# Row LSTM after a group norm: the second row of both halves issued in the steady order instead of in sequences of its own

## The chip, the core and the metric

The kernel runs on one core of one Trainium2 chip. A time is the device time of one execution in microseconds (us). Before the change the median of three runs is 2032.22 us (2031.02 to 2032.76). One more execution was taken with the hardware profiler; it took 2030.92 us, and its trace spans 2029.1 us.

## What is computed

The input x has 8 images of 96 channels, 128 rows and 128 columns, all in 32-bit floats. It is group-normalised; a masked convolution along the row gives four gate inputs for each pixel; then an LSTM walks down the rows, and its hidden state h is convolved along the row with three taps. The result is added to x. Cut to what matters:

```python
its = conv(groupnorm(x), W_is * mask) + b_is          # 96 -> 384 channels, 1x3, along the row
def step(carry, row_in):
    h, c = carry
    gates = conv(h, W_ss) + b_ss + row_in             # 96 -> 384 channels, 3 taps, along the row
    f, i, o = sigmoid(...), sigmoid(...), sigmoid(...)
    g = tanh(...)
    c_new = f * c + i * g
    h_new = o * tanh(c_new)
    return (h_new, c_new), h_new
x = x + scan(step, rows of its)
```

Rows depend on each other through h and c. The images don't.

## The kernel before

**Halves and steps.** The eight images are two halves of four. A *half step* n is one row of one half: n = 2 x row + half, so steps 0 and 1 are the first row of both halves, steps 2 and 3 the second row, and the last step is 255. Step n needs h of step n-2. While one half's gates are computed, TensorE works on the other half. "h(n)", "vf(n)" and so on below are what belongs to step n.

**What a step consists of.** The 384 gate channels are three banks of PSUM, A, B and C, of 128 channels. Even and odd pixels of a row are kept apart, and each bank has two halves of 256 columns for them. The operands of a step are made from h of the row above: `F` (`difference`, tile vf, on VectorE, L585), `S` (`total`, tile vs, VectorE, L573) and `D` (`shifted`, tile vd, GpSimd, L589). TensorE then writes, for each bank, the products of x (`P`, `Q`, weights wx; `E`, weights wt) and of h (`1` from vs, `2` from vf, `0` and `3` from vd); all are line L442. In between, ScalarE copies half a bank out with the bias (`cp`, L508) and VectorE adds and subtracts it back (`lo` L512, `hi` L516), so that even and odd pixels come out of fewer products; only then do `0`, `3` and `E` go into the bank. The gates follow: `ta` (tanh, ScalarE, L520), `si` (sigmoid, ScalarE, L527), `fg` (f times c, VectorE, L532), `gt` (i times g, L537), `ce` (L547), `th` (tanh of c, ScalarE, L552) and `ou` (h, VectorE, L560). `re` (L607, GpSimd) adds h to x for the output.

**The order is written out by hand.** Each engine executes its instructions in the order in which the code lists them. `do(n, names)` lists parts of step n. In a name, `'` means step n-1, `+` step n+1 and `*` step n+2; `F`, `S` and `D` always mean the operands of two steps later. A part that is already listed is skipped. From step 4 on, every step is listed by one string, `PERIOD`:

```python
    PERIOD = (
        "2A hiC' siA' D'' 1B 1A taA' 2B fg' 3C' 1A 0C' re'' taB' 2A 2B EC' 1B cpA 0C' 2C W loA cpB "
        "3C' 1C siB' loB PB+ QA+ hiA taCb' 2C hiB taCa' 0A gtb' 1C siC' gta' EA 0B ceb' cpC 3A PA+ "
        "cea' thb' PC+ 3B loC tha' QC+ oub' EB oua' QB+ 3A F' 3B 0A S' 0B"
    )
```

It mixes products of step n with the gates of step n-1 and with the x products of step n+1. `W` lists GpSimd's preparation of later rows of x (`prepare(n-1)`: normalising images into the tiles xs and hx, L297, L315, L316). Gates with a trailing a or b are done for the even or the odd pixels alone.

**Row groups.** With `by_lanes=True` products are listed in *pieces* of 64 of the 128 contraction rows: a product of h is two pieces and is named twice in `PERIOD`; a product of x has its operand twice in the tile, and one piece is enough. The two 64-row groups of the array work side by side. `Lanes.take` chooses a group so that both get as many pieces; where a bank was last written from the other group, `lanes.wait` has TensorE wait for that product. Without `by_lanes`, a product of h is one matmul over 128 rows (`whole`), and one of x goes to a group fixed by its bank (`own`).

**Around the change.** The statistics of x take the first 134 us or so. Steps 0 and 1 and the products of step 2 are listed by hand in the lines above L936 and are not touched. Then come L936 to L945, which list steps 2 and 3; the two `PERIOD` calls in them add what was still missing (GpSimd's `prepare`, residuals, and the products P and Q of step 4). At L946 the loop over steps 4 to 255 begins.

Of the kernel before, what the change touches and what calls it, by code (L numbers as in the profile page):

```python
# [21 lines left out]
def kernel(  # L22
# [335 lines left out]
    last = NT * NH - 1  # L358
# [299 lines left out]
    def prepare(n):  # L658
        if n not in worked:
            worked.add(n)  # L660
            for part, *args in work(n):
                part(*args)

    def finish(n):
        prepare(n)
        row, s = divmod(n, NH)
        k, r = divmod(row, R)
        if r == R - 1:
            store(s, k, R - 1 if k + 1 == NB else 0, R)
            if k + 2 < NB:  # L670
                load(s, k + 2)
        elif r == R - 2 and k + 1 == NB:
            store(s, k, 0, R - 1)
# [4 lines left out]
# [5 lines that stand above are left out]
# [10 lines left out]
    def half_step(n):  # L693
        if n not in steps:
            steps[n] = HalfStep(n)
        return steps[n]

    def do(n, names, by_lanes=False):

        for name in names.split():  # L700
            if name == "W":
                prepare(n - 1)
                continue
            at = n
            for mark, offset in (("'", -1), ("+", 1), ("*", 2)):
                at += offset * name.count(mark)
                name = name.replace(mark, "")
            pixels = PIXELS[name[-1]] if name[:-1] in SPLIT and name[-1] in PIXELS else ()
            whole_name = name[:-1] if pixels else name
            tile_ = whole_name[-1] if whole_name[-1] in order else ""  # L710
            part = whole_name[: len(whole_name) - len(tile_)]

            if part in ("S", "F", "D"):
                at += NH
            if not 0 <= at <= last:
                continue
            step = half_step(at)
            if name in step.done or whole_name in step.done:
                continue
            if by_lanes and (part in OWN or part in H_PRODUCTS) and (  # L720
                at < last or part in ("P", "Q") or (part, order[tile_]) in step.halves
            ):
                if step.piece(part, order[tile_]):
                    step.done.add(name)
                continue
            step.done.add(name)
            getattr(step, PARTS[part])(*([order[tile_]] if tile_ else []), *pixels)
            if by_lanes and part == "re":
                finish(at)
# [120 lines left out]
    n = m = 0  # L850
# [82 lines left out]
    finish(0)  # L933
    do(1, "gt th 0+A 3+A 0+B 3+B 0+C 3+C ou F S D re")
    finish(1)
    do(2, "taA siA taB fg siB taC")  # L936
    do(3, "2A 1A 2B 1B PC QC 2C 1C cpA cpB loA loB hiA hiB")
    do(2, "gt ce siC th")
    do(3, "cpC")
    do(2, "ou")  # L940
    do(3, "loC hiC EA EB EC 0A 3A 0B 3B 0C 3C")
    do(2, "F S D")
    do(2, PERIOD, by_lanes=True)
    do(3, PERIOD, by_lanes=True)
    do(3, "taA siA taB fg siB taC gt ce siC th ou F S D")  # L945
    for n in range(4, last + 1):  # L946
        do(n, PERIOD, by_lanes=True)
    do(last, "cpA cpB cpC loA hiA loB hiB loC hiC 0A 3A EA 3B 0B EB", by_lanes=True)
    do(last, "taA siA 0C 3C EC siB taB fg taC siC gt oua' oub' re'", by_lanes=True)
# [63 lines left out]
```

## Time and profile before

| | before |
|---|---|
| median of three runs | 2032.22 us |
| the runs | 2031.02 to 2032.76 us |
| profiled execution | 2030.92 us |
| its span | 2029.1 us |
| busy: TensorE, VectorE, ScalarE, GpSimd | 95%, 75%, 74%, 72% of the span |
| TensorE, instructions in the trace | 16912 matmuls |
| mean granted TensorE clock | 0.997 of full speed |

The profile comes from one execution. PE is TensorE's matmuls, PEld its weight loads, DVE VectorE, ACT ScalarE, POOL GpSimd, SPq the queue that issues DMAs. One product of the code shows as two matmul records. A line of the timeline has the start in us from the span's start, the time until the last of the merged instructions ends, the engine, the line, the operation, the tile written and the tiles read, partitions x elements, and how many records are merged; a bracket names the idle time before it and what ended it. `64*128` is a matmul over 64 contraction rows, `128*128` over all 128.

### The profile page before, as it was taken

The page shows a single profiled execution, that of the slowest core. Times are in us where ns is not written, and L with a number is a line of the kernel's source. Part 1 is how long each engine was busy: PE and PEld are TensorE (multiplying, and loading weights), DVE is VectorE, ACT ScalarE, POOL GpSimd, SP SyncE. Part 2 cuts the span into 40 slices and gives each one's busy share as a digit, 9 for nine tenths or more (in the row PEclk, how much of TensorE's full clock was granted, in tenths as well). Part 3 has the DMA queues.
Part 4 walks back from the last instruction along what each step waited for, and adds up shares of the span by engine and source line. Part 5 has one row for each costly group of instructions (what it writes and reads, how often), then busy time and mean ns, then how long its engine had stood idle before and what let it go on. Part 6 is the DMA issues. An engine that isn't in the chain of part 4 may idle for free.

```text
span 2029.1 us, 44784 instructions
## 1 busy us (share of the span) xinstructions
PE 1925.3 (95%) x16912; PEld 1830.0 (90%) x16912; DVE 1526.6 (75%) x3990; ACT 1493.7 (74%) x3157; POOL 1469.6 (72%) x1712
## 2 busy tenths in 40 slices
PE   0289999999999999999999999999999999999998
PEld 0267999999999999999999999999999999999997
DVE  5776777777777777777777777777777777777776
ACT  4775777777777777777777777777777777777776
POOL 3347777777777777777777777777777777777752
PEclk9999999999999999999999999999999999999999
DMA  9993433443343344333433443343344334434411
GB/s 378 424 314 79 108 95 95 115 115 94 79 100 98 92 114 115 100 84 89 113 91 100 116 115 85 82 106 95 95 115 115 95 79 99 105 91 109 115 32 32
DMA packets 103382, 237.11 MB, mean 117 GB/s; under 512 B 5952, under 2 KB 8896, under 8 KB 97280
## 3 DMA queue, kind: packets, MB, share of 16 engines
q1 hardware_dynamic: 103168, 234.25, 42.5%
q8 instruction: 135, 2.21, 0.5%
q14 instruction: 79, 0.65, 0.1%
HBM read 183.90 MB, written 50.33 MB: 115 GB/s over the span
## 4 chain that ended last, share of the span: by engine, by line
PE 92%; DMA 4%; ACT 2%; DVE 1%; issue 0%; SPq 0%; POOL 0%; DVEq 0%; POOLq 0%
PE ps L442 92%; DMA piece<-in_x_dram 3%; DMA xs<-in_x_dram 1%; ACT piece L216 1%; PE ps L174 0%; ACT piece L217 0%; DVE bst L876 0%; ACT g L520 0%; ACT hx L295 0%; ACT piece L295 0%; DVE hx L560 0%; DVE ps L516 0%; ACT ps L527 0%; ACT xs L216 0%; ACT xs L217 0%
## 5 line engine op out<-in xcount | busy, mean ns | idle before, releaser
L442 PE MATMUL ps<-vd,wl 64*128 64x256 f32 (+1 forms) x6084 | 1390.3, 380 | 0.3
L442 PEld LDWEIGHTS ps<-vd,wl 64*128 64x128 f32 (+1 forms) x6084 | 1028.3, 187 | 46.4 <-issue 2.1
L442 PE MATMUL ps<-vs,wm 64*128 64x256 f32 (+1 forms) x3046 | 773.8, 380 | 5.0 <-POOL vs L573 4.2
L442 PE MATMUL ps<-vf,wm 64*128 64x256 f32 (+1 forms) x3046 | 765.5, 377 | 1.1 <-DVE vf L585 1.1
L527 ACT ACTIVATE ps<-ps 96x512 f32<-96x512 f32 x766 | 441.7, 577 | 356.3 <-PE ps L442 348.0
L442 PE MATMUL ps<-xs,wx 64*128 64x256 f32 x3080 | 637.2, 378 | 11.2 <-POOL xs L315 11.1
L589 POOL TENSOR_TENSOR vd<-hx 128x512 f32<-128x512 f32 x257 | 266.2, 1036 | 398.4 <-PE ps L442 391.5
L442 PEld LDWEIGHTS ps<-xs,wx 64*128 64x128 f32 x3080 | 493.3, 188 | 15.1 <-POOL xs L315 11.5
L520 ACT ACTIVATE g<-ps 32x512 f32<-32x512 f32 x1019 | 468.0, 482 | 30.7 <-PE ps L442 10.4
L442 PEld LDWEIGHTS ps<-vf,wm 64*128 64x128 f32 (+1 forms) x3046 | 475.4, 187 | 13.1 <-DVE vf L585 1.5
L442 PEld LDWEIGHTS ps<-vs,wm 64*128 64x128 f32 (+1 forms) x3046 | 460.6, 186 | 21.6 <-POOL vs L573 5.3
L512 DVE TENSOR_TENSOR ps<-m,ps 128x256 f32<-128x256 f32 x768 | 325.7, 425 | 192.2 <-ACT m L508 181.9
L442 PE MATMUL ps<-xs,wt 64*128 64x256 f32 x1530 | 453.1, 377 | 2.5 <-DVE ps L516 2.4
L508 ACT ACTIVATE m<-ps,wl 128x256 f32<-128x256 f32 x766 | 360.9, 473 | 92.1 <-PE ps L442 85.6
L532 DVE TENSOR_TENSOR ps<-ps,c 96x512 f32<-96x512 f32 x254 | 176.7, 696 | 238.9 <-PE ps L442 231.0
L607 POOL TENSOR_TENSOR x<-x,hx 96x512 f32<-96x512 f32 x255 | 330.0, 1294 | 6.8 <-DVE hx L560 6.7
L516 DVE TENSOR_TENSOR ps<-m,ps 128x256 f32<-128x256 f32 x768 | 300.8, 422 | 1.3 <-PE ps L442 1.2
L442 PEld LDWEIGHTS ps<-xs,wt 64*128 64x128 f32 x1530 | 279.7, 186 | 15.5 <-DVE ps L516 3.2
L316 POOL TENSOR_TENSOR xs<-xw 128x512 f32<-128x512 f32 (+1 forms) x254 | 270.0, 1063 | 0.0
L297 POOL TENSOR_SCALAR hx<-x,rstd,nmr 32x384 f32<-32x384 f32 (+2 forms) x312 | 224.6, 720 | 32.9 <-DMA x<-in_x_dram 0.8
L297 POOL TENSOR_SCALAR xw<-xr,rstd,nmr 128x512 f32<-128x512 f32 x252 | 205.0, 814 | 7.2 <-DVE nmr L289 6.7
L537 DVE TENSOR_TENSOR g<-ps,g 96x256 f32<-96x256 f32 (+1 forms) x505 | 188.7, 413 | 5.4 <-ACT g L520 5.4
(91 smaller groups left out, 1218.2 us busy)
## 6 DMA issues: line engine op xcount, KB each, us to landing
xr<-in_x_dram SPq DMA_DIRECT2D x124, 512.0 KB, 6.6
x<-in_x_dram SPq DMA_DIRECT2D x63, 768.0 KB, 6.0
out_dram<-x SPq DMA_DIRECT2D x62, 768.0 KB, 4.6
xs<-in_x_dram SPq DMA_DIRECT2D x30, 1024.0 KB, 12.5
piece<-in_x_dram SPq DMA_DIRECT2D x16, 1024.0 KB, 12.3
x<-in_x_dram SPq DMA_DIRECT2D x62, 256.0 KB, 3.2
xs<-in_x_dram SPq DMA_DIRECT2D x4, 512.0 KB, 8.2
out_dram<-x SPq DMA_DIRECT2D x2, 576.0 KB, 3.7
```

The costliest lines, as they stand in the source:

```text
L297: return engine.tensor_scalar(dst, src, scale, shift, ALU.mult, ALU.add)
L316: nc.gpsimd.tensor_sub(differences, strided(xw[:, 0, :], 0, [(W + 1, n), (J, 2), (1, J)]), strided(xw[:, 0, :], J + 1, [(W + 1, n), (0, 2) ...
L442: made = nc.tensor.matmul(self.ps[a][:, bass.ts(half, HB)][:, cols], weights[rows, bass.ts(a, P)], rhs[rows, cols], start=new, stop=False, ...
L508: nc.scalar.activation(self.m1[a], m1, AF.Identity, bias=column)
L512: nc.vector.tensor_add(self.ps[a][:, 0:HB], self.m1[a], self.ps[a][:, HB:])
L516: nc.vector.tensor_sub(hi, self.m1[a], hi)
L520: nc.scalar.activation(self.part(g, lo, hi, t), self.part(ps, lo, hi, t), AF.Tanh)
L527: nc.scalar.activation(gate, gate, AF.Sigmoid)
L532: nc.vector.tensor_mul(f, f, self.c)
L537: nc.vector.tensor_mul(to, i, g)
L589: diff = nc.gpsimd.tensor_sub(self.operand("vd", 2)[:, :, lo:hi], strided(h, 1, [(BH * JP - 1, 2), (JP, hi - lo), (1, J)]), strided(h, 0, ...
L607: (nc.gpsimd if 2 * row + s < last else nc.vector).tensor_add(xo, xo, self.h)
```

## The change

The hand-written sequences of steps 2 and 3 (L936 to L945) go, and the loop over `PERIOD` starts at step 2:

```diff
     finish(0)
     do(1, "gt th 0+A 3+A 0+B 3+B 0+C 3+C ou F S D re")
     finish(1)
-    do(2, "taA siA taB fg siB taC")
-    do(3, "2A 1A 2B 1B PC QC 2C 1C cpA cpB loA loB hiA hiB")
-    do(2, "gt ce siC th")
-    do(3, "cpC")
-    do(2, "ou")
-    do(3, "loC hiC EA EB EC 0A 3A 0B 3B 0C 3C")
-    do(2, "F S D")
-    do(2, PERIOD, by_lanes=True)
-    do(3, PERIOD, by_lanes=True)
-    do(3, "taA siA taB fg siB taC gt ce siC th ou F S D")
-    for n in range(4, last + 1):
+    for n in range(2, last + 1):
         do(n, PERIOD, by_lanes=True)
```

What stays to be listed at n = 2 is little, since the products of step 2 are already listed above: `W` and the products `PC+` and `QC+` of step 3. At n = 3 the products of step 3 are listed in 64-row pieces, mixed with the gates of step 2 and with P and Q of step 4. The last products of step 3's bank C (`3C'`, `0C'`, `EC'`), its `hiC'` and its gates come at n = 4, mixed with the products of step 4. The end of the kernel (L948 on) has the same text. The number of arithmetic operations is the same except that twelve 128-row products become twenty-four 64-row pieces, and that the gates taC, gt, ce, th and ou of steps 2 and 3 are split into even and odd pixels.

## Prediction

> A *cycle* n runs here from TensorE's first product of vf(n) to its first of vf(n+1): one half step in the loop.
>
> **What bounds the kernel now.** First the page: what carries the chain that ended last.
>
> ```profile
> PE 92%; DMA 4%; ACT 2%; DVE 1%; issue 0%; SPq 0%; POOL 0%; DVEq 0%; POOLq 0%
> ```
>
> TensorE carries it nearly throughout. The chain in order of time shows where it doesn't, after the statistics:
>
> ```profile
> 157.85 0.44 DVE ps L516
> 158.33 5.85 PE ps L442 x18
> ...
> 174.31 26.45 PE ps L442 x215
> ...
> 206.41 1807.24 PE ps L442 x16244
> ```
>
> The long stretch runs at 1807.24/16244 = 0.111 us a record; in the middle one it is 26.45/215 = 0.123. Just ahead of 158.33 TensorE waited for VectorE. The TensorE timeline of that place, with a first record of later cycles:
>
> ```profile
> 151.16 0.70 PE L442 MATMUL ps<-vf,wm 128*128 128x256 f32 x2 [1.06 <-DVE vf L585]
> ...
> 158.33 0.70 PE L442 MATMUL ps<-xs,wt 64*128 64x256 f32 x2 [2.43 <-DVE ps L516]
> 158.96 4.54 PE L442 MATMUL ps<-vd,wl 128*128 128x256 f32 x12
> 163.43 2.33 PE L442 MATMUL ps<-xs,wx 64*128 64x256 f32 x12
> 165.59 0.38 PE L442 MATMUL ps<-vf,wm 64*128 64x256 f32 x1
> ...
> 173.04 0.48 PE L442 MATMUL ps<-vf,wm 64*128 64x256 f32 x1
> ...
> 182.29 0.48 PE L442 MATMUL ps<-vf,wm 64*128 64x256 f32 x1
> ...
> 190.54 0.38 PE L442 MATMUL ps<-vf,wm 64*128 64x256 f32 x1
> ```
>
> Step 3 begins at 151.16, step 4 at 165.59: 14.43 us. Cycles 4, 5 and 6 then take 7.45, 9.25 and 8.25 (differences of the starts). Cycle 7 starts at 190.54, cycle 8 at 197.89, and two later starts, 1005.61 and 1012.94, are 7.33 apart: the steady cycle. So the early steps are the only place with something to win. In stretches (length, busy time and count of PE, PEld, DVE, ACT, POOL, then clock, DMA share, GB/s):
>
> ```profile
> 156.00:159.00 3.00, 0.67 (x3) 0.34 (x3) 2.21 (x6) 0.99 (x2) 0.40 (x1) 1.00 1.05 207
> 159.00:163.00 4.00, 4.00 (x12) 3.24 (x12) 0.70 (x1) 1.79 (x4) 3.73 (x5) 0.57 0.09 20
> 163.00:166.00 3.00, 2.85 (x19) 1.65 (x19) 1.37 (x2) 2.07 (x4) 1.34 (x2) 1.00 0.00 0
> ```
>
> After the idle stretch the clock is 0.57 for 4 us, so the twelve vd records take 0.38 us each instead of 0.22 (24 records in 5.45 us at 144.65): 12 x 0.16 = 1.9 us. With the idle 2.43 that is 4.3 us; the rest above a steady cycle, 14.43 - 7.33 - 4.3 = 2.8, is products in one row group alone or in another order than the steady one (PC and QC: 1.13 us for 4 records; P and Q of step 4: 2.33 us for 12).
>
> [...] records at 165.59 and 165.60 overlap. [...] S, 0.42 us elsewhere, took 1.29 beside GpSimd's L316 (first line VectorE, second GpSimd):
>
> ```profile
> 205.06 1.29 DVE L573 TENSOR_TENSOR vs<-hx 128x256 f32<-128x256 f32 x1
> ```
> ```profile
> 204.76 1.32 POOL L316 TENSOR_TENSOR xs<-xw 128x512 f32<-128x512 f32 x1
> ```
>
> **The change part by part.** The instruction order of the two programs (no time in it) says how the pieces move. From step 3 on, the changed program's cycle n has the pieces, row groups and group waits of the old program's cycle n+1: 3 is like old 4, 4 like old 5, 5 like old 6, later ones steady, 33 pieces each. So the 14.43 us go, and one more steady cycle comes. Step by step, from the same 151.16:
>
> 1. *PC and QC of step 3* come ahead of 2A. Their bank is that of step 1's A, last read by taA at 147.64 at the latest, and x row 1 was ready by 143.33. So two pieces run in the idle 1.06 us before 151.16: nothing added. Without that cover: 2 x 0.43 = 0.86, as their group wait keeps them apart.
>
> 2. *Cycle 3.* TensorE alone would take old cycle 4's 7.45: 158.61. Old cycle 4 found vs ready; here S(3) ends at 151.43, so the pieces of `1` start some 0.35 later: 158.96. The other limit is F(4). In old cycle 4 ScalarE's first copies came 2.25 us after the start; here 151.16 + 2.25 + 0.35 = 153.76. Then ScalarE in its order: cpA, cpB to 154.6; siB 0.57, taC 0.65, siC 0.57 to 156.4; cpC when its products are in (old +5.16), 156.7 to 157.15; th 0.73 to 157.9; on VectorE `ou` to 158.3, F 0.43. TensorE could start at about 158.98. siA, taA, taB lie ahead of cpA and end by 151.5; fg, lo, hi, gt, ce lie beside ScalarE. Both limits meet at 159.0.
>
> 3. *GpSimd.* Its idle 156.39 to 159.08 is filled: own_image(0,2) (0.80 + 0.64 + 1.06 with gaps, to 159.0) and two L297 (1.70) now stand ahead of D(4), which ran at 159.08. D(4) then ends at about 161.8. Old cycle 5 used vd 5.83 after its start; here 159.4 + 5.8 = 165.2, a cover of 3.4 us. But own_image's L316, about 157.9 to 159.0, meets F(4) at 158.35. The case at 150.45 cost F 0.23 (0.65 against 0.42), the one at 205.06 cost S 0.87. From nothing to 0.9; I take 0.5, since L316 would end some 0.6 after F could start: cycle 4 starts at 159.5. Before, F(4) and S(4) ran at 158.19 beside an idle GpSimd.
>
> 4. *Cycles 4 and 5* take old 9.25 and 8.25: 168.75, 177.0. Old cycle 5 is long because the pieces of `1B` come late in a doubly loaded group: cpB ran 4.4 us after the start (177.45), against 2.8 in the steady state (1008.39 after 1005.61), and the gates hang on it; the same groups come again. hiC(3) is now near its user `3C`, as in the steady order. GpSimd keeps up: D(4), re 1.29, own_image 2.6, two L297 1.7 end at 167.4; S(5) comes near 169.0. Then D(5), re and two images (5.2) to 176.8, and F(6) comes at about 176.7: again an edge where up to 0.9 may be lost, for which I add nothing.
>
> 5. *Cycle 6* takes 7.35, so cycle 7 starts at 184.35 instead of 190.54: **6.2 us earlier**.
>
> 6. *DMAs.* None is added, and SyncE's order is the same. Transfers fill 137 to 159 before; own_image(0,2) reads rows that landed by 148.27 and the shared rows of x come from a transfer ahead of the last ones of that burst. load_rows(0,2) leaves some 6 us earlier, into an idle queue. The next steps repeat: the clash at 205.06 belongs to two images in one step's work and should come again, earlier.
>
> 7. *Steady state.* 248 cycles keep their 7.33. Row groups are swapped against equal n, but they alternate from step to step anyway.
>
> Sum against the profiled execution: 2030.92 - 6.2 = 2024.7. That execution stands 1.3 below the median, so for the median 2032.22 - 6.2 = **2026.0 us**, own range 2024 to 2028.5.
>
> **Rivals.**
>
> *More is won.* Cycles 4 and 5 run at 7.33 (2.8 less), as their feeds differ from old 5 and 6, or no clash comes (0.5). Up to 3.3 more: 2022.7. Against it: identical groups and waits.
>
> *The gain is eaten by the gates.* F(4) is the tight place, since both limits meet there. If step 2's gates wait behind step 3's copies longer than I count, each us late is a us lost. cpA, cpB and cpC are the three places; 0.9 each (a group wait that holds a bank back, as cpB's 1.6 in old cycle 5) plus a second clash of 0.9 is 3.6: 2029.6. For it: ScalarE executes in order. Against it: the steady order does this every 7.33 us, and its cpB-to-F time (1008.39 to 1012.75, 4.36) is that in my sum.
>
> *Slower: swapped row groups cost in the steady state.* If half 0 with the upper group, as in the changed program's odd pattern, were slower, the price is per cycle times 248. It eats the gain at 6.2/248 = 25 ns a cycle and shows as slower from 41 ns; at 60 ns: 2026.0 + 14.9 = 2040.9. Against it: old even and odd cycles have opposite groups and both last 7.33; GpSimd and VectorE write operands on all 128 partitions alike.
>
> *No change of order* is excluded: the programs differ as told.
>
> **How the numbers follow.** Main case 0.68; more won 0.10; gain eaten 0.15; slower or something unseen, as a late GpSimd or a clock drop in the waits (1.9 us once), 0.07. Range 2022.5 to 2031.0: the first two and most of the third. A measurement of this kernel tells about 0.2%, 4.06 us: faster needs less than 2028.2. Main case nine in ten, all of more won, little of the eaten: 0.74; same 0.19; slower 0.07.
>
> **What would show it.** Right: no idle 2.4 us of TensorE and no clock below 1.00 between 155 and 166; first vf of cycle 4 at 159 to 160, then gaps near 9.25, 8.25 and 7.35; D(4) after two L297; steady cycle 7.33. Wrong: cycle 4 starting after 162 (the gates), gaps near 7.33 at once (more won), a steady cycle off 7.33 by tens of ns (groups), or VectorE waiting for GpSimd again and again.

## The result, and the profile after

The changed kernel takes 2024.95 us (median of 8 runs, 2023.52 to 2027.04); the kernel before, measured beside it, 2030.92 us (8 runs, 2030.27 to 2032.76). The ratio is 0.9969, with a 95% interval of 0.9958 to 0.998: **faster by 6 us**, 0.3%, with 4 to 8.5 us inside the interval. The forecast was 2026.0, own range 2024 to 2028.5; it started from a median of three runs, 2032.22, which the eight runs put 1.3 us lower.

The profiled execution took 2027.04 us with a span of 2025.2, only 3.9 us less than before. Its statistics phase, which the change doesn't touch, was longer: cycle 3 starts at 153.54 instead of 151.16. In the profiles below, all with the same code up to step 3, this start lies anywhere between 149.9 and 153.6. So cycles are compared by their lengths, not by their places.

The page's summary of the chain that ended last, and some of its pieces in order of time (start, length, engine, tile, line, records):

```profile
PE 93%; DMA 4%; ACT 2%; DVE 1%; issue 0%; SPq 0%; POOL 0%; DVEq 0%; POOLq 0%
```
```profile
147.04 6.09 PE ps L442 x26
153.17 3.15 PE ps L442 x20
156.36 40.34 PE ps L442 x320
201.09 1.22 DVE vs L573
202.35 1807.47 PE ps L442 x16243
```

No VectorE piece stands ahead of the stretch from 156.36 any more, and that stretch has 40.34/320 = 0.126 us a record against 1807.47/16243 = 0.111 in the long one: the chain never leaves TensorE there, but TensorE isn't at its steady pace either. In this chain `S`, which came late once before (205.06), still does once. In stretches, with the columns of the same view of before (PEclk is the third number from the right):

```profile
156.00:159.00 3.00, 2.94 (x20) 2.31 (x19) 2.59 (x8) 2.62 (x7) 2.81 (x5) 1.00 1.07 194
159.00:163.00 4.00, 4.00 (x33) 3.34 (x31) 3.24 (x7) 2.07 (x5) 3.71 (x5) 1.00 0.62 127
163.00:166.00 3.00, 2.99 (x26) 2.39 (x24) 1.12 (x2) 1.55 (x4) 2.92 (x3) 1.00 0.02 5
```

TensorE is busy 9.93 of these 10 us, where it was busy 7.52 before, and at full clock throughout. The starts of the cycles in TensorE's timeline:

```profile
153.54 0.70 PE L442 MATMUL ps<-vf,wm 64*128 64x256 f32 x2
...
161.11 0.48 PE L442 MATMUL ps<-vf,wm 64*128 64x256 f32 x1
...
162.13 0.70 PE L442 MATMUL ps<-vs,wm 64*128 64x256 f32 x3
...
170.36 0.48 PE L442 MATMUL ps<-vf,wm 64*128 64x256 f32 x1
...
178.92 0.48 PE L442 MATMUL ps<-vf,wm 64*128 64x256 f32 x1
...
186.37 0.48 PE L442 MATMUL ps<-vf,wm 64*128 64x256 f32 x1
```

Cycles 3 to 6 take 7.57, 9.25, 8.56 and 7.45 us, together 32.83; before they took 14.43, 7.45, 9.25 and 8.25, together 39.38. That is 6.55 us less (forecast 6.2). After cycle 12 nothing differs: from F(13) to the end there are 1794.3 us before and 1794.4 after, and F is 7.33 us apart in the loop (1000.97 and 1008.30).

### The profile page after: what moved, and what is told of

Its sections match the earlier page's. It is cut to its first block, busy times and chain, and to the rows that moved or that the text cites. A ratio compares the mean times of both kernels' runs of the same rounds, so it can differ in the third digit from the quotient of the medians.

```text
span 2025.2 us, 44842 instructions
## 1 busy us (share of the span) xinstructions
PE 1923.3 (95%) x16936; PEld 1831.0 (90%) x16936; DVE 1529.1 (76%) x3996; ACT 1494.9 (74%) x3161; POOL 1473.1 (73%) x1712
## 4 chain that ended last, share of the span: by engine, by line
PE 93%; DMA 4%; ACT 2%; DVE 1%; issue 0%; SPq 0%; POOL 0%; DVEq 0%; POOLq 0%
PE ps L442 92%; DMA piece<-in_x_dram 3%; DMA xs<-in_x_dram 1%; ACT piece L216 1%; PE ps L174 0%; ACT piece L217 0%; DVE bst L876 0%; ACT hx L295 0%; ACT piece L295 0%; DVE hx L560 0%; ACT xs L216 0%; ACT xs L217 0%; SPq L864 0%; PE pv L251 0%; DVE ps L516 0%
## 5 line engine op out<-in xcount | busy, mean ns | idle before, releaser
L520 ACT ACTIVATE g<-ps 32x256 f32<-32x256 f32 (+1 forms) x1021 | 468.6, 482 | 26.7 <-PE ps L442 6.3
L316 POOL TENSOR_TENSOR xs<-xw 128x512 f32<-128x512 f32 (+1 forms) x254 | 270.9, 1067 | 0.0
L297 POOL TENSOR_SCALAR hx<-x,rstd,nmr 32x384 f32<-32x384 f32 (+2 forms) x312 | 225.8, 724 | 33.2 <-DMA x<-in_x_dram 1.1
L297 POOL TENSOR_SCALAR xw<-xr,rstd,nmr 128x512 f32<-128x512 f32 x252 | 205.6, 816 | 7.1 <-DVE nmr L289 6.5
L537 DVE TENSOR_TENSOR g<-ps,g 96x256 f32<-96x256 f32 x507 | 189.0, 413 | 3.8 <-ACT g L520 3.8
```

The lines of the kernel that those rows point to most:

```text
L297: return engine.tensor_scalar(dst, src, scale, shift, ALU.mult, ALU.add)
L316: nc.gpsimd.tensor_sub(differences, strided(xw[:, 0, :], 0, [(W + 1, n), (J, 2), (1, J)]), strided(xw[:, 0, :], J + 1, [(W + 1, n), (0, 2) ...
L520: nc.scalar.activation(self.part(g, lo, hi, t), self.part(ps, lo, hi, t), AF.Tanh)
L537: nc.vector.tensor_mul(to, i, g)
```

## The experiments

Two things were open. Which parts of the old 14.43 us did the change win back, and is that the same in every execution? And why do two cycles of 9.25 and 8.56 us come after it, where the steady one takes 7.33? The theory was the prediction's: the idle 2.43 us and the clock fall behind it, both gone, and then row groups that make two cycles long. Rivals: that the clock fall has nothing to do with the idle time; that the long cycles come from a late `S`, from GpSimd, or from the gates.

All numbers in one table. F-F is the time from the start of F(3) to that of F(13) in the profile; medians are of timed runs, the ratio is to the kernel before measured on the same chip.

| kernel | cycle 3 | 4 | 5 | 6 | F-F | median us | ratio, 95% interval |
|---|---|---|---|---|---|---|---|
| before | 14.43 | 7.45 | 9.25 | 8.25 | 84.38 | 2030.92 | |
| before, again (a) | 14.39 | 7.45 | 9.25 | 8.25 | 84.27 | one run | |
| before, again (b) | 16.02 | 7.46 | 9.25 | 8.25 | 86.06 | one run | |
| before, again (c) | 15.82 | 7.45 | 9.25 | 8.25 | 85.70 | one run | |
| e5, order as before | 12.75 | 7.45 | 9.24 | 8.26 | 82.73 | 2030.96 | 1.0 (0.9991 to 1.0008) |
| e2, idle filled | 12.75 | 7.46 | 9.25 | 8.25 | 82.68 | 2028.73 | 0.9993 (0.9984 to 1.0001) |
| e3, EC later | 11.03 | 7.45 | 9.25 | 8.25 | 80.95 | 2027.02 | 0.9983 (0.9976 to 0.9989) |
| e8, groups level at 5 | 15.91 | 7.45 | 8.48 | 7.44 | 84.39 | 2029.01 | 0.9992 (0.9983 to 1.0) |
| after | 7.57 | 9.25 | 8.56 | 7.45 | 77.93 | 2024.95 | 0.9969 (0.9958 to 0.998) |
| e4, GpSimd work later | 7.57 | 9.25 | 8.25 | 7.34 | 83.28 | 2029.65 | 0.9995 (0.9986 to 1.0004) |
| e7, gates earlier | 7.56 | 9.25 | 8.59 | 7.44 | 77.94 | 2024.09 | 0.9966 (0.9954 to 0.9979) |
| e1, groups level at 4 | 8.29 | 7.44 | 7.33 | 7.69 | 77.06 | 2022.72 | 0.9964 (0.9951 to 0.9977) |
| e6, level, ScalarE helps | 7.57 | 7.84 | 7.33 | 8.11 | 75.73 | 2023.41 | 0.9964 (0.9951 to 0.9976) |

### What the old cycle 3 was made of

**Fill the idle time.** In the kernel before, five products that nobody reads are written into bank B of step 4 between `EB` and `EC`.

```diff
-    do(3, "loC hiC EA EB EC 0A 3A 0B 3B 0C 3C")
+    do(3, "loC hiC EA EB")
+    half_step(4).take_bank(1)
+    for i in range(5):
+        nc.tensor.matmul(half_step(4).ps[1][:, 0:256], wt[0][:, 0:P], wt[0][:, 0:256],
+                         start=True, stop=True, skip_group_check=True)
+    do(3, "EC 0A 3A 0B 3B 0C 3C")
```

> The kernel before, with five matmuls that nobody reads in the 2.43 us in which TensorE waited ahead of step 3's EC. Theory (the clock fell because of the idle stretch, and that is worth 1.9 us): the clock stays at 1.00 between 159 and 163 us, the twelve vd records take 2.6 us instead of 4.54, cycle 3 takes 12.5 instead of 14.43. Rival (the clock falls anyway, or the time goes into another wait): 14.2 to 14.6.

TensorE's timeline of this run, the filling and the vd records after it:

```profile
155.11 2.43 PE L944 MATMUL ps<-wl 128*128 128x256 f32 x10
...
158.25 2.86 PE L442 MATMUL ps<-vd,wl 128*128 128x256 f32 x12
```

The twelve vd records take 2.86 us instead of 4.54, 0.24 each, and cycle 3 takes 12.75 instead of 14.43: the clock fall was worth 1.68 us in the first profile, where the prediction had 1.9. That looked like the answer until the next run.

**A repeat that was not meant as one.** It was to choose the row groups afresh at step 4 of the kernel before:

```diff
     for n in range(4, last + 1):
+        if n == 4:
+            lanes.taken = [0, 0]
         do(n, PERIOD, by_lanes=True)
```

> The kernel before, with the count of pieces per row group set level once, before step 4. If the groups make the long cycles in the old order too (that cycles 4 and 5 of the changed kernel are cycles 5 and 6 of the old one), old cycles 5 and 6, 9.25 and 8.25 us, fall to 7.3 to 7.7, and F(3) to F(13) takes 81.0 to 82.2 us instead of 84.38. If they belong to the old sequence of step 3 and what it leaves late, they stay and it takes 84.4. What a level count is worth would then be the same before and after the change, up to what GpSimd takes back.

The count is level there anyhow, so not one instruction moved, and the run says nothing on row groups. It is the kernel before, measured and profiled once more (its ratio of 1.0, 0.9991 to 1.0008, shows what the measurement gives for no difference). Its timeline:

```profile
157.94 0.70 PE L442 MATMUL ps<-xs,wt 64*128 64x256 f32 x2 [2.43 <-DVE ps L516]
158.57 2.86 PE L442 MATMUL ps<-vd,wl 128*128 128x256 f32 x12
```

The same idle 2.43 us, and no clock fall behind it. So 12.75 in the run before could have been chance, and the first profile's drop too. Three more profiles of the unchanged kernel were taken.

> The kernel before, unchanged, profiled again. Theory, that the clock after the idle 2.43 us falls in some executions and not in others: cycle 3 takes either 14.4 us, with twelve vd records in 4.5 us, or 12.75 us, with these in 2.9 us, and the idle 2.43 us is there in both. Rival, that the drop belongs to the first profile alone: 12.75 in all three repeats.

> The same again: 14.4 us or 12.75 us for cycle 3, the idle 2.43 us in both; by the rival 12.75.

> The same again: 14.4 us or 12.75 us for cycle 3, the idle 2.43 us in both; by the rival 12.75.

Cycle 3 took 14.39, 16.02 and 15.82 us. The idle 2.43 us is in all three. The rival, that the first drop was the exception, fell at once, but two of the three values are in neither theory. The timeline of repeat b, and the stretch behind its pause:

```profile
158.03 1.21 PE L442 MATMUL ps<-xs,wt 64*128 64x256 f32 x2 [2.43 <-DVE ps L516]
159.18 5.49 PE L442 MATMUL ps<-vd,wl 128*128 128x256 f32 x12
```
```profile
158.00:165.00 7.00, 6.97 (x16) 4.78 (x18) 1.34 (x3) 2.63 (x5) 5.07 (x6) 0.51 0.14 29
```

Here the clock is halved for nearly 7 us, though TensorE is busy 6.97 of them. Added up from stretches of 1 us (the share of full clock missing in each, doubled), the time at half clock between 149 and 169 is 3.40 us in the first profile, 3.42 in repeat a, 6.84 in b, 6.82 in c, 6.84 in e8 (below, which is the kernel before up to step 5), and none in e5. These are no, one and two units of 3.41 us. In the first profile the clock changes at 111.64, 115.06, 125.30, 128.71, 159.43, 162.84 and 2026.52 us. The distances, 3.41, 10.24, 3.41, 30.72, 3.41 and 1863.68, are 1, 3, 1, 9, 1 and 546 times 3.413. In the profile of the changed kernel it changes at 111.37, 118.20, 128.44, 131.85 and 2022.83; the distances there, 6.83, 10.24, 3.41 and 1890.98, are 2, 3, 1 and 554 times 3.413.

Set against the pause, the profiles lie in order. The stretch of 1 us in which the clock fell, in the first profile, a, b, c and e8 (a clock of 0.72, with 0.50 in the next stretch, means that it fell 0.44 us into it):

```profile
159.00:160.00 1.00, 1.00 (x5) 0.81 (x5) 0.00 (x0) 0.00 (x0) 0.92 (x1) 0.72 0.28 57
160.00:161.00 1.00, 1.00 (x5) 0.80 (x4) 0.00 (x0) 0.90 (x2) 0.92 (x3) 0.55 0.07 25
158.00:159.00 1.00, 0.97 (x2) 0.50 (x2) 0.64 (x2) 0.00 (x0) 0.21 (x1) 0.53 0.85 156
156.00:157.00 1.00, 0.00 (x0) 0.00 (x0) 0.97 (x3) 0.14 (x1) 0.00 (x0) 0.93 1.06 203
157.00:158.00 1.00, 0.02 (x1) 0.02 (x1) 0.97 (x4) 0.00 (x0) 0.00 (x0) 0.86 1.05 205
```

The pauses of these five end at 158.33, 158.27, 158.03, 157.36 and 157.98. Where one unit followed, the clock fell 1.10 us (first profile) and 1.83 us (a) after the end of the pause. Where two followed, it fell 0.04 us after that end (b), or 0.25 us (e8) and 0.50 us (c) ahead of it. In e5, where the pause ended at 157.94, it stayed at 1.00 from 149 to 169. So with a fall 1.10 us or more behind the end of the pause the clock stayed down for one unit, with one at 0.04 us or less for two. The length of the pause alone doesn't decide it: that is 2.43 us in all six. This is an order in a few profiles, read afterwards; what the rule is stays open.

Over these six profiles of the same code cycle 3 is 12.75 plus 1.68, 0, 1.64, 3.27, 3.07 and 3.16: on average 2.1 us is lost to the clock. The timed runs agree: with the idle time filled (e2) the median is 1.97 us lower than the 2030.7 of before in the same series, though its interval just reaches 1. The filling itself saves no time by TensorE's timeline (12.75 with it, 12.75 without it and without a drop). That the clock stayed at 1.00 from 156 to 164 in every kernel without the pause (after, e1 to e4, e6, e7) fits, and so does a drop of one unit, 3.42 us, in e4 (below) after a pause of 3.98 us that came up elsewhere and ended at 186.98. No run moved the pause against the clock's changes on purpose.

**Undo only the pause, by order.** In the old sequence `EC` waits for `hiC` on VectorE, and all products behind it wait with it (in the first profile `EC` began at 158.33, after 2.43 us of idle time, and the vd records at 158.96). Here the products that don't need it go ahead:

```diff
-    do(3, "loC hiC EA EB EC 0A 3A 0B 3B 0C 3C")
+    do(3, "loC hiC EA EB 0A 3A 0B 3B EC 0C 3C")
```

> The kernel before, with one edit: in the sequence of step 3, EC is listed behind 0A 3A 0B 3B instead of ahead of them. Theory (the stall was only EC standing first in TensorE's queue while hiC was not done; other products were ready): eight records of 0.22 us fill 1.8 us of the idle time and the clock stays up, so cycle 3 takes 10.0 to 11.0 us instead of 14.43, and the gain that is left to the change is 2 to 3 us. Rival (the wait moves to other operands, D or lo): 12.5 or more.

TensorE's timeline of this run:

```profile
155.79 1.99 PE L442 MATMUL ps<-vd,wl 128*128 128x256 f32 x8
158.29 0.70 PE L442 MATMUL ps<-xs,wt 64*128 64x256 f32 x2 [0.51 <-DVE ps L516]
```

The pause shrinks from 2.43 to 0.51, the clock stays at 1.00, and cycle 3 takes 11.03, just above the 10.0 to 11.0 that were expected. Against 12.75 this is 1.72 us; with the clock's average 2.1 added it is 3.8 us; the medians differ by 3.7 (2030.7 to 2027.02). So, by the medians, more than half of the change's gain was to be had by moving one name in one line (its interval is 2.2 to 4.9 us, that of the change 4 to 8.5). The rest of the old cycle 3, 11.03 - 0.51 - 7.57 = 2.95 us, is what the steady order takes away besides: PC and QC (1.13 us in the old timeline), which now begin at 152.41, ahead of the cycle, and products in whole or one-group form. No run takes these apart.

### What makes two cycles long

**Not the late S and not GpSimd.** In the changed kernel, VectorE and GpSimd at the edge between cycles 3 and 4:

```profile
160.45 0.43 DVE L585 TENSOR_TENSOR vf<-hx 128x256 f32<-128x256 f32 x1
160.79 1.29 DVE L573 TENSOR_TENSOR vs<-hx 128x256 f32<-128x256 f32 x1
```
```profile
160.46 1.34 POOL L316 TENSOR_TENSOR xs<-xw 128x512 f32<-128x512 f32 x1
161.91 1.77 POOL L297 TENSOR_SCALAR hx<-x,rstd,nmr 32x512 f32<-32x512 f32 x2
163.76 1.04 POOL L589 TENSOR_TENSOR vd<-hx 128x512 f32<-128x512 f32 x1
```

L316 met S(4), which took 1.29 instead of 0.42; the first products of vs began at 162.13, 1.02 us after those of vf. Is that the excess of cycle 4? The work of GpSimd was moved away:

```diff
-        own(0, 2) + shared(0, 1, 0, 1),
+        [],
...
-        own(1, 2) + shared(1, 1, 0, 1),
+        own(1, 2) + shared(1, 1, 0, 1) + own(0, 2) + shared(0, 1, 0, 1),
```

> The changed kernel, with GpSimd's work of step 2 (one image of x and two shared parts) done in step 5's place, so that nothing of GpSimd runs beside F(4) and S(4). Both theories: S(4) takes 0.42 us instead of 1.29. Theory A (the row groups set the length of cycle 4, and the late S is absorbed): cycle 4 stays at 9.1 to 9.3. Theory B (the late S is paid in full): cycle 4 falls to 8.3 to 8.5. Step 5's place gets 4.3 us more of GpSimd, so cycles 6 to 8 may be up to 1 us longer; the verdict is taken from cycles 3 and 4 alone.

VectorE and TensorE of this run:

```profile
157.18 0.42 DVE L573 TENSOR_TENSOR vs<-hx 128x256 f32<-128x256 f32 x1
...
186.50 0.42 DVE L573 TENSOR_TENSOR vs<-hx 128x256 f32<-128x256 f32 x1 [4.25 <-POOL hx L297]
```
```profile
157.50 0.48 PE L442 MATMUL ps<-vf,wm 64*128 64x256 f32 x1
...
166.75 0.48 PE L442 MATMUL ps<-vf,wm 64*128 64x256 f32 x1
...
175.00 0.38 PE L442 MATMUL ps<-vf,wm 64*128 64x256 f32 x1
```

S(4) takes 0.42, and cycle 4 takes 9.25 as before: a delay of 0.87 us in S vanished in a cycle that something else made long. Cycle 5 falls from 8.56 to 8.25. The edit took away both collisions at its edges, S(5) (0.86 us) and F(6) (0.68 us); the 0.26 us by which F(6) was long are most of the 0.31, but no run takes the two apart. The moved work comes back later as a 4.25 us wait of S(7) for GpSimd (and 3.98 us of TensorE's idle time, with a clock fall behind it), far more than the 1 us expected. It takes nearly all of the gain: F-F is 83.28.

**Row groups.** The changed kernel enters step 4 with uneven counts of pieces (by the code, 16 and 14), and single pieces go to the group that has fewer until the counts are level. One line sets the counts level:

```diff
     for n in range(2, last + 1):
+        if n == 4:
+            lanes.taken = [0, 0]
         do(n, PERIOD, by_lanes=True)
```

> The changed kernel, with the count of pieces per row group set level once, before step 4, so that cycle 4 starts in the steady pattern of row groups. Theory (the two long cycles come from the row groups that the imbalance left by cycle 3 brings about): cycles 4 and 5, now 9.25 and 8.56 us, fall to 7.4 to 8.0, the upper end if GpSimd's two images in one step hold one of them; from the first product of step 3 to that of step 7 it takes 30.0 to 31.3 us instead of 32.8. Rival (the long cycles are a start-up of gates and GpSimd, whatever the groups): 9.2 and 8.5 stay, 32.8.

TensorE's timeline, and VectorE's:

```profile
158.64 0.70 PE L442 MATMUL ps<-vf,wm 64*128 64x256 f32 x2
...
166.08 0.38 PE L442 MATMUL ps<-vf,wm 64*128 64x256 f32 x1
...
173.41 0.38 PE L442 MATMUL ps<-vf,wm 64*128 64x256 f32 x1
...
181.10 0.38 PE L442 MATMUL ps<-vf,wm 64*128 64x256 f32 x1
```
```profile
157.25 1.33 DVE L585 TENSOR_TENSOR vf<-hx 128x256 f32<-128x256 f32 x1
...
189.69 0.42 DVE L573 TENSOR_TENSOR vs<-hx 128x256 f32<-128x256 f32 x1 [1.43 <-POOL hx L297]
```

Cycles 4 and 5 take 7.44 and 7.33. The same work is listed in the same order, with only the groups chosen otherwise, and with them the waits of one group for the other: these are what made 9.25 and 8.25. But of the 3.0 us only 0.87 is left at F(13) (77.06 against 77.93). The shorter cycles bring VectorE to GpSimd before the latter is done: 1.43 us of waiting ahead of S(8), and a collision in which S(6) took 0.88. (S(9), 1.28 or 1.29, is long in every kernel here.) And F(4) met L316 for 0.9 us, where in the changed kernel S(4) did. GpSimd in this run:

```profile
157.24 1.06 POOL L316 TENSOR_TENSOR xs<-xw 128x512 f32<-128x512 f32 x1
```

That is not the edit's doing, which comes only at step 4. L316 began 0.01 us ahead of F(4) here (157.24 and 157.25), and F(4) took 1.33 us and L316 1.06; in the changed kernel it began 0.01 us behind F(4) (160.46 and 160.45), and F(4) took 0.43 and L316 1.34. Which of them was long hung on 0.01 us, and it is worth 0.72 us of cycle 3 (8.29 against 7.57).

The same in the old order, one step later, where the counts are uneven:

```diff
     for n in range(4, last + 1):
+        if n == 5:
+            lanes.taken = [0, 0]
         do(n, PERIOD, by_lanes=True)
```

> The kernel before, with the count that chooses the row groups set level ahead of step 5 instead of carried over. Theory, that uneven row groups and not the work make the 9.25 and the 8.25 us cycle in the old order too: cycle 4 stays 7.45, cycles 5 and 6 fall to 7.3 to 7.8 each, and the start of F(13) comes 1.0 to 2.7 us earlier after F(3) than before, less what a late GpSimd takes back. Rival, that the two long cycles are a consequence of the order of step 4's last copies and gates: 9.25 and 8.25 stay, and nothing is won. Cycle 3 is as before in both.

TensorE's, VectorE's and GpSimd's lines:

```profile
174.16 0.48 PE L442 MATMUL ps<-vf,wm 64*128 64x256 f32 x1
...
182.64 0.70 PE L442 MATMUL ps<-vf,wm 64*128 64x256 f32 x2
...
190.08 0.44 PE L442 MATMUL ps<-vf,wm 64*128 64x256 f32 x1
```
```profile
181.39 1.20 DVE L585 TENSOR_TENSOR vf<-hx 128x256 f32<-128x256 f32 x1
```
```profile
181.24 1.06 POOL L316 TENSOR_TENSOR xs<-xw 128x512 f32<-128x512 f32 x1
```

Cycle 6 falls from 8.25 to 7.44, within the expectation. Cycle 5 falls only to 8.48, above the 7.3 to 7.8 expected: F(6) came 7.23 us after the cycle's start (8.58 in the first profile, 173.04 to 181.62), met L316 and took 1.20 instead of 0.42. If these 0.78 are paid in full, the cycle is 7.70 without them; that is an estimate, no run removes them. Against repeats b and c, whose clock fell for as long, F(13) comes 1.67 and 1.31 us earlier after F(3); the medians differ by 1.61, with an interval that reaches 1. By the cycles the theory holds; the rival, that 9.25 and 8.25 follow from the order of the last copies, would have left both, and neither stayed.

**Give GpSimd less.** The changed kernel with level groups, where ScalarE does the shared part of two images at a time (L295 in place of L297, after the steps named in AFTER; `shared` of these images is taken out of GpSimd's lists), and the residual of step 1 stands behind D(4):

```diff
...
+    AFTER = {3: (0, (0, 1)), 4: (0, (2, 3)), 6: (1, (0, 1)), 7: (1, (2, 3))}
     for n in range(2, last + 1):
+        if n == 4:
+            lanes.taken = [0, 0]
+            do(n, "D''")
+            half_step(1).residual()
         do(n, PERIOD, by_lanes=True)
+        if n in AFTER:
+            half, images = AFTER[n]
+            for j in images:
+                normalise_shared(nc.scalar, half, 1, j, 0, R)
```

> The changed kernel with the level count, and with GpSimd relieved: the shared parts of x of steps 2, 3, 5 and 6 are normalised on ScalarE at the end of the next step's listing, and the residual of step 1 is done behind D(4). Theory (with level groups GpSimd is what is late: F(4) 0.9 us, S(6) 0.5, S(8) 1.4 in the level kernel): F(3) to F(13) takes 74.8 to 75.8 us, against 77.06 with the level count alone and 77.93 in the changed kernel. Rival (ScalarE has no room; two more instructions hold up siA and the gates): 0.5 us or more is lost in each of four cycles, 76.5 to 79.

ScalarE's line, and one of VectorE's:

```profile
159.54 1.73 ACT L295 ACTIVATE hx<-x,nmr,rstd 32x512 f32<-32x512 f32 x2
```
```profile
175.63 1.29 DVE L573 TENSOR_TENSOR vs<-hx 128x256 f32<-128x256 f32 x1
```

F-F is 75.73, another 1.33 less and 2.2 less than after; 0.72 of the 1.33 is cycle 3, in which L316 now ends before F(4). The work isn't all done in idle time: the chain that ended last passes through such a pair of L295 at 167.40, 182.84 and 190.18, and cycle 4 takes 7.84 where e1 has 7.44 (no run shows whether the two belong together). Two collisions are left, S(6) and S(9), 0.87 us each. In the timed runs neither e1 (2022.72) nor e6 (2023.41) can be told from the changed kernel: the three intervals lie over each other. By F-F they are better by 0.87 and 2.2 us, at most 0.1%, and no run here proves it.

### What sets F(4)

In the changed kernel the gates siB and taC of step 2 stand behind step 3's first copies on ScalarE. ScalarE's timeline of after:

```profile
155.91 0.84 ACT L508 ACTIVATE m<-ps,wl 128x256 f32<-128x256 f32 x2 [2.17 <-PE ps L442]
156.64 0.59 ACT L527 ACTIVATE ps<-ps 96x512 f32<-96x512 f32 x1
...
158.82 0.47 ACT L508 ACTIVATE m<-ps,wl 128x256 f32<-128x256 f32 x1 [0.33 <-PE ps L442]
```

To see whether the gates or TensorE's own products decide, they were listed ahead of the loop:

```diff
+    do(2, "taA siA taB fg siB taC")
     for n in range(2, last + 1):
         do(n, PERIOD, by_lanes=True)
```

> The changed kernel with the old first line of step 2 kept ahead of the loop, so that ScalarE does siB, taC of step 2 in the 2.2 us in which it waits for cpA. If F(4) sets cycle 3 (7.57 us), it comes 0.6 to 1.2 us earlier and cycle 3 falls to 7.1 to 7.4. If TensorE's own work sets it too, as the prediction had it (7.45 alone), it stays at 7.4 to 7.6. Behind cycle 4 nothing should change either way.

ScalarE's timeline of this run:

```profile
153.76 0.84 ACT L508 ACTIVATE m<-ps,wl 128x256 f32<-128x256 f32 x2 [0.84 <-PE ps L442]
...
156.67 0.47 ACT L508 ACTIVATE m<-ps,wl 128x256 f32<-128x256 f32 x1 [1.60 <-PE ps L442]
```

In this run ScalarE took siB and taC in the listed order, at 151.73 and 152.33 and so ahead of cpA and cpB (in after at 156.64 and 157.24, behind them). ScalarE now waits 1.60 us for cpC's products instead of 0.33, and cpC comes 5.27 us after the cycle's start, as before the edit (5.28). Cycle 3 stays at 7.56. So not siB or taC but TensorE, through cpC, then `th` and `ou`, sets F(4), which comes 6.9 us after the cycle's start in both: the two limits that the prediction found meeting hang on the same products. The rival that the gates eat the gain had nothing to eat. Since F(4) didn't move, the run doesn't show whether an earlier F(4) would shorten the cycle. There is some slack: in e1 F(4) ended 0.9 us later in its cycle, and cycle 3 grew by 0.72 only.

## Why the prediction was right

**What bounds the kernel.** The order and the numbers of the parts were right on average, and in part by luck. The idle 2.43 us and the clock's "1.9" were won. The clock's part is 1.68 in that execution, and 0, 1.6 or 3.1 to 3.3 in others; the average of six, 2.1, is near the value used. Had the first profile been like e5, the same reasoning would have priced the change at 4.5, and like b at 7.8 us. One execution can't price a clock fall. The starting level held luck too: the 1.3 us added for the median of three runs were gone in the median of eight. Without them the forecast would have been 2024.7, against 2024.95 measured.

**PC and QC (step 1).** Nothing added, as forecast.

**Cycle 3 (steps 2 and 3).** Forecast 8.34, measured 7.57. Of the 0.77, 0.5 is the collision of L316 with F(4), which met S(4) instead; 0.23 is the 0.35 for the late S(3), of which at most 0.12 appeared (7.57 against the old 7.45); the rest is rounding. cpA came 2.37 us after the start (forecast 2.60), cpC 5.28 (5.54). The place of the collision was foreseen, and which instruction it hits can't be, as it hung on 0.01 us: e1 shows what it costs when it hits F, 8.29 instead of 7.57. So the term is 0 or 0.7 by chance, and the 0.5 was a value between.

**D(4) behind two L297.** It ran from 163.76, 10.2 us after the cycle's start, where the forecast has 9.6. As forecast, TensorE did not wait for it.

**Cycles 4 and 5 (step 4).** 9.25 exactly; 8.56 instead of 8.25. The term "I add nothing" for the edge at F(6) was wrong by up to 0.31. The forecast named the reason, a doubly loaded group that holds `1B` and so cpB back. In cycle 4 cpB came 4.41 us after the start, as in old cycle 5 (165.52 against 161.11); with level groups (e1) it came after 2.89. That the groups, with their waits, make the length is shown by e1 and e8.

**Cycle 6 (step 5).** 7.45 for 7.35. The sum: 0.77 less, 0.31 and 0.1 more, so 6.55 for 6.2; misses of both signs cancel in part.

**DMAs and the steady state (steps 6 and 7).** As forecast. The 243 cycles from 13 on, with the groups of the halves exchanged, cost nothing that shows (1794.3 and 1794.4 us from F(13) to the end). The rival of the slower steady state is out.

**The rival "more is won"** was no part of this change, but e1 shows that it was real: the 2.8 us were there, and the groups held them. It also shows why they are hard to take: 0.87 us remain, after GpSimd's share and the 0.72 that fell to chance.

The profile's 6.55 and the medians' 5.97 agree well within the interval. By the average cycle 3 of the six profiles (14.9) the gain should be near 7 us.

## What to carry to other kernels

TensorE took its products in the listed order (before: `EC` at 158.33, the vd records from 158.96; e3: eight of these from 155.79, `EC` at 158.29). In such a hand-written sequence look for the one name that waits, and for what stands behind it without needing it: moving one product's name won 3.7 of the 6 us by the medians. A pause of TensorE can cost more than its length (here 2.43 us, and 0 to 3.3 us more in six profiles), so price it over several profiles. And where a delay is found, ask whether the cycle that holds it has slack: 0.87 us of a late operand cost nothing here, and of 3 us of shorter cycles 0.87 was left.

## What the hardware showed

- With a pause of 2.43 us TensorE's clock fell to one half for 0, 3.41 or 6.83 us, in six profiles with the same code up to step 5 (once, twice and three times), the longest while TensorE was busy almost throughout (6.97 of 7 us). In the profiles of before and after the changes of the clock lie whole multiples of 3.413 us apart (1, 3, 9 and 546 in the one, 1, 2, 3 and 554 in the other).
- VectorE's F and S took longer when they met GpSimd's L316: 0.42 us became 1.29 (S, in after and before) and 1.33 (F, in e1), and L316 itself took 1.34 instead of 1.06 beside S(4). The longest of these collisions cost nearly the same, 0.87 to 0.91; whether that reaches TensorE is another matter: 0.87 us at S(4) did not lengthen cycle 4, 0.9 us at F(4) lengthened cycle 3 by 0.72.
- Uneven use of the two 64-row groups and the waits that come with it turned a cycle of 7.44 us into one of 9.25, with the same products listed in the same order.
